# Where the rounded part of a product is subtracted: VectorE in SBUF, or TensorE inside the PSUM bank

## The chip, the cores and the metric

The kernel runs on one core of a Trainium2 chip. Its time is the device time of one execution in microseconds (us). The core has five engines that run their own instruction streams and meet at semaphores: TensorE (PE in the profile, its weight loads PEld), VectorE (DVE), ScalarE (ACT), GpSimd (POOL) and SyncE (SP). TensorE writes its products to PSUM[...]; VectorE and ScalarE read them there.

## The reference

`x` is 16 x 1024 x 256, `adj` a sparse 1024 x 1024 matrix (a few entries per row, the diagonal always). Cut to what matters:

```python
pre_u = einsum('bud,dk->buk', h, W1[:d])
pre_v = einsum('bvd,dk->bvk', h, W1[d:])
S  = sigmoid(einsum('buvk,ko->buvo', relu(pre_u[:, :, None] + pre_v[:, None] + b1), W2)[..., 0] + b2)
a  = einsum('buv,bud->bvd', S * adj, h)
m  = einsum('uv,bud->bvd', adj, h) * h
z  = beta1 * h + beta2 * (a @ Wa + ba) + beta3 * (m @ Wm + bm)
```

Each edge (u, v) has a gate per batch, from the sum of a row of `pre_u` and a row of `pre_v`; the gated and the plain neighbour rows are summed per v and multiplied by two weight matrices.

## The kernel before

**Tiling.** The kernel gathers only existing edges. The batches are 4 groups of 4, the nodes 8 tiles of 128, so there are 32 blocks (group, tile). A block is ten steps, two windows (`w`) of 64 nodes with five lists of 128 edges each. Within a block I count steps from 0 to 9; the code calls the step `s = n % 10` and the block `k = n // 10`. In one step, for 128 edges and 4 batches at once:

- GpSimd fetches the 128 neighbour rows from a table in DRAM (`fetch`, L496), six buffers ahead: 1024 columns of `pre_u` and 1024 of `h`;
- TensorE spreads the block's own `pre_v` rows over the edges, by a 0/1 matrix `mark` (`expand`, L569): `pc = mark.T @ X`, two matmuls of 512 columns. It does so two steps ahead, in two buffers;
- VectorE adds both (`gate`, L601), and applies relu, W2 and the sum over columns, batch by batch (L606, four times);
- ScalarE takes the sigmoid (L609), and scales the edge matrix `left` with it (L612, four times; L579 prepares the next `left`);
- TensorE sums the neighbour rows into accumulators (`aggregate`, L623).

**X and its two parts.** [...] So a row of `pre_v` is stored in two parts: a rounded one and what rounding took away, the low part. `X` is a tile of 128 partitions and two windows. For window 0, partitions 0 to 63 hold the window's rounded rows and partitions 64 to 127 its low parts; for window 1 it is the other way round. `mark` has the one of an edge in both places, so the product adds both parts. `halves(k)` builds `X` for block k while block k - 1 runs:

- per half (512 of 1024 columns) TensorE forms `b1 + h @ w_v` in a PSUM tile `p` (`add_row`, L431, and `half_product`, L427);
- ScalarE copies it to `X` rounded (L461) and to `low` as it is (L462);
- VectorE subtracts the rounded part from `low` (L463), for all 1024 columns at once;
- ScalarE copies the rounded rows of window 1 to their place (L465) and the low parts to theirs (L468, twice).

It is a generator: each `yield` hands on to the next step at which it is called, and those steps are 0, 2, 3, 5 and 6 of block k - 1.

**The order of the work.** It is written out by hand: the main loop (L745) emits each engine's instructions in program order, and `after(step, f)` puts work off to a later step. [...] In a step, TensorE gets the accumulate of the step before, the `expand` for two steps ahead, and then what belongs to this step:

- step 0: half 0 of `halves`; step 1: four transposes of an accumulator (`turn_over`, L641; ScalarE copies the result to `LT`, L644); step 2: half 1;
- steps 3 to 6: the end of the block before (`block_end`: products with `w_a` and `w_m`, L672, copied to `z` by L675);
- steps 7 and 9: transposes again.
- In a list of further steps (`at`, L730), a half of `rows`: `pre_u` of a later group (`w_u`, L427), copied to `tab` by ScalarE (L443) and stored to the table. In blocks 7 to 16 and 18 to 23 one of these is in step 1, behind the transposes and behind what `halves` does there. After block 23 there are none.

**PSUM.** All these products, the transposes, and `p`, live in tiles named `misc` (`small`, L220), for which there are two banks. A new `misc` tile waits until a bank's last reader is done. `pc` and the accumulators have banks of their own.

Of the kernel before, what the change touches and what calls it, by code (L numbers as in the profile page):

```python
# [7 lines left out]
FP = mybir.dt.float32  # L8
FR = mybir.dt.float32r
I32 = mybir.dt.int32  # L10
AF = mybir.ActivationFunctionType
ALU = mybir.AluOpType
AX = mybir.AxisListType
P = 128
# [3 lines left out]
def kernel(  # L18
# [42 lines left out]
    nc = tc.nc  # L61
# [5 lines left out]
    GD = GB * D  # L67
    W = 64
    NW = P // W
# [35 lines left out]
    def fixed(shape, name, dt=FP):  # L105
        return const.tile(shape, dt, name=name)
# [8 lines left out]
    upto = fixed([P, E], "upto")  # L115
# [3 lines left out]
    row = rows32[:, 0:1]  # L119
# [64 lines left out]

    unit = fixed([P, P], "unit", FR)
    nc.vector.tensor_scalar(unit, upto[:, :P], 0.0, None, ALU.is_ge)
    edge = fixed([P, 1], "edge")
    nc.vector.tensor_scalar(edge, inw, 0.0, None, ALU.is_equal)

# [21 lines left out]
    one = main.enter_context(tc.tile_pool(name="one", bufs=1))  # L211
# [8 lines left out]
    def small(name):  # L220
        return psm.tile([P, 512], FP, name="misc")
# [157 lines left out]
    def fetch_val(n):  # L379

        for i, j in wanted[:n]:
            nc.gpsimd.indirect_dma_start(  # L382
                out=val[:, i, j:j + 1], out_offset=None, in_=adj_flat,
                in_offset=bass.IndirectOffsetOnAxis(ap=vidx[:, i, j:j + 1], axis=0),
                bounds_check=N * N - 1, oob_is_err=False)
        del wanted[:n]
# [12 lines left out]
    def after(step, f):  # L399
        due.setdefault(step, []).append(f)  # L400
# [23 lines left out]
    def half_product(p, hT, wt, h, begun):  # L424
        for bb in range(2):
            for i in range(DC):
                nc.tensor.matmul(p[:, bb * D:(bb + 1) * D], hT[:, 2 * h + bb, i, :], wt[:, i, :],  # L427
                                 start=(i == 0 and not begun), stop=(i == DC - 1), skip_group_check=begun)

    def add_row(p, parts):  # L430
        nc.tensor.matmul(p, unit, parts.unsqueeze(1).to_broadcast([P, 2, D]),  # L431
                         start=True, stop=False, skip_group_check=True)
# [18 lines left out]

    def halves(k):
        X = cuts[k] = big.tile([P, NW, GD], FR, name="X")
        low = one.tile([P, GD], FP, name="low")
        for h in range(2):
            step = yield
            c = slice(2 * h * D, (2 * h + 2) * D)
            p = small("p")
            add_row(p, b1_p)
            half_product(p, hTs[order[k]], w_v, h, True)  # L460
            nc.scalar.copy(X[:, 0, c], p)  # L461
            nc.scalar.copy(low[:, c], p)  # L462
        after(step + (2 if k else 1), lambda: nc.vector.tensor_tensor(low, low, X[:, 0, :].bitcast(FP), ALU.subtract))  # L463
        yield
        nc.scalar.copy(X[W:, 1, :], X[W:, 0, :].bitcast(FP))  # L465
        for w in range(NW):
            yield
            nc.scalar.copy(X[(1 - w) * W:(2 - w) * W, w, :], low[w * W:(w + 1) * W])  # L468

    engines = mybir.EngineType  # L470
    main.enter_context(tc.manual_schedule(
# [2 lines left out]
    def do(step):  # L474
        for f in due.pop(step, ()):
            f()
# [10 lines left out]
    BS = NG * NT  # L487
# [6 lines left out]
    def fetch(n):  # L494
        k, g, vt, w, j = where(n)
        nc.gpsimd.indirect_dma_start(  # L496
            out=fetched[n % NF], out_offset=None, in_=table[g],
            in_offset=bass.IndirectOffsetOnAxis(ap=uidx[:, vt * NW + w, j:j + 1], axis=0),
            bounds_check=N - 1, oob_is_err=False)
# [23 lines left out]
    for t, turns_ in enumerate(script):  # L523
        step = t - 100
# [48 lines left out]
    def left_adj(n):  # L573
        k, g, vt, w, j = where(n)
        i = vt * NW + w
        m = len(QUARTERS[j])
        o = max(2 * j - 1, 0)
        lefts[n] = wk.tile([P, 2, GB, 2, V], FP, name="left")
        nc.scalar.activation(lefts[n][:, :m, :, 0, :], onehot[:, i, o:o + m, :].unsqueeze(2).to_broadcast([P, m, GB, V]),  # L579
                             AF.Copy, scale=val[:, i, j:j + 1])  # L580
# [33 lines left out]
    def aggregate(n):  # L614
        k, g, vt, w, j = where(n)
        left, f = lefts.pop(n), fetched[n % NF]
        for i, q in enumerate(QUARTERS[j]):
            h, r = divmod(q, 2)
            first = j == h * MID and r == 0
            if first:  # L620
                accs[h] = psa.tile([P, 2, D], FP, name=f"acc{h}")
            for b in range(GB):
                nc.tensor.matmul(accs[h][b * 2 * V:(b + 1) * 2 * V, r, :],  # L623
                                 left[:, i, b].rearrange("p k v -> p (k v)"), f[:, GD + b * D:GD + (b + 1) * D],
                                 start=first, stop=(j == q + 1), skip_group_check=True)


    def half_end(n, q):

        evs[q] = one.tile([P, 2, D], FP, name=f"ev{q}")  # L630
        nc.scalar.copy(evs[q], accs.pop(q))  # L631
# [113 lines left out]
    for n in range(total + 2):  # L745
        k, s = divmod(n, T)
        if 1 <= n <= total:
            aggregate(n - 1)
            fetch_val(2)
            if n - 1 + NF < total:  # L750
                fetch(n - 1 + NF)
            if n % TW in (0, MID + 1):
                half_end(n - 1, 0 if n % TW else 1)
        if n < total:
            gate(n)
            if n + 1 < total:
                left_adj(n + 1)
        if n % TW == 1 and n // TW + 1 < total // TW:
            load_mark(n // TW + 1)
        do(n)  # L760
        if n + 2 < total:
            expand(n + 2)
        if n == 1:
            w_a = load_weights(Wa, "w_a", nc.sync)
            w_m = load_weights(Wm, "w_m", nc.sync)
            bias = load_rows(bm, D, "bias", nc.sync)
            ba_b = load_rows(ba, D, "ba_b", nc.sync)
            be1 = load_rows(beta1, 1, "be1", nc.sync)
            be2 = load_rows(beta2, 1, "be2", nc.sync)
            be3 = load_rows(beta3, 1, "be3", nc.sync)  # L770
            after(10, scale_late)
        if s == 0 and 0 < k < BS:
            hbs[k - 1] = big.tile([P, GB, D], FP, name="h_blk", bufs=1)
            g, vt = order[k - 1]
            nc.sync.dma_start(hbs[k - 1], x_rows[vt * P:(vt + 1) * P, g * GB:(g + 1) * GB, :])
        if n == total - 6:
            hbs[BS - 1] = hts.tile([P, GB, DC, P], FP, name="hT").rearrange("p b c n -> p b (c n)")
            for v, m, f in tails:
                for h, o in tail_rows(x, v, m, f):
                    nc.sync.dma_start(h, o)  # L780
        for i in advance.get(n, ()):
            next(made[i], None)
        if n in start_list:
            running.append([made[start_list[n]], True, n])
            piece_of(running[-1], n)
        fill(n, False)
        if (s == 1 and 0 < k < BS) or n == total:
            turn_over(k - 1, 1, 1, n)
        if s in (3, 4, 5, 6) and 0 < k < BS:
            if s == 3:  # L790
                end = block_end(k - 1)
                next(end)
            go(end, n)
        if s == 7 and k < BS:
            turn_over(k, 0, 0, n)
            turn_over(k, 0, 1, n)
        if s == 9 and k < BS:
            turn_over(k, 1, 0, n)
        if n == total - 2:
            end = tail(tails[:2], n)  # L800
            next(end)
        elif n == total - 1:
            go(end, n)
        elif n >= total:
            end = tail([tails[2 + n - total]], n)
            next(end)
            go(end, n)
            go(end, n)
        if k + 1 < BS and s in (0, 2, 3, 5, 6):
            if s == 0:  # L810
                parts = halves(k + 1)
                next(parts)
            go(parts, n)
        if n in loads:
            if loads[n] in begun and loads[n][0] == 1:
                aside_.remove(loads[n])
            load_hT(loads[n])
            if loads[n] not in begun:
                copy_h(loads[n])
                begun.add(loads[n])  # L820
        if n in at:
            if at[n] != last:
                last = at[n]
                piece = rows(last)
                next(piece)
            go(piece, n)
        if n == 120:
            nc.gpsimd.partition_all_reduce(longest, rest, P, bass_isa.ReduceOp.max)
            after(n + 12, count_rest)
# [7 lines left out]
    with tc.If(any_left > 0):  # L837
        with ExitStack() as s2:
# [3 lines left out]
            for vt in range(NT):  # L842
# [55 lines left out]
                for b in range(B):  # L898
# [7 lines left out]
                    for k, w in enumerate((w_m, w_a)):  # L906
                        for c in range(DC):
                            nc.tensor.matmul(pz, lt[:, k, c, :], w[:, c, :],
                                             start=(k == 0 and c == 0), stop=(k == 1 and c == DC - 1))
# [34 lines left out]
```

## Time and profile before

| | us |
|---|---|
| median of three runs | 1175.09 |
| lowest, highest | 1167.80, 1177.88 |
| span of the profiled execution | 1165.8 |
| first gate to last gate | 71.6 to 1145.4 |
| a block, by the gates: blocks 0 to 5 | 37.6 to 42.7 |
| blocks 7 to 23 | 31.3 to 37.9 |
| blocks 24 to 30 | 31.3 to 31.9 |

The profiled execution's own time is not given apart from its span; its span lies 9.3 us below the median of the runs and 2.0 below the lowest. A row of the timeline has start, length, engine, line, operation, tiles written and read, shapes and count; in brackets stands how long the engine was idle before it, and which instruction ended that. Matmuls are pipelined: each row's length counts until the last result, so the distance of two starts, not the length, is what one costs TensorE.

### The profile page before, as it was taken

To read this page: it belongs to the slowest core of one execution; us is meant where nothing else is said; L and a number is where in the kernel's file an instruction comes from. 1 tells how busy PE (TensorE), PEld (TensorE's weight loads), DVE (VectorE), ACT (ScalarE), POOL (GpSimd) and SP (SyncE) were. 2 spreads that over 40 slices of the span, in tenths; PEclk is the share of its full clock that TensorE was granted. 3 is DMA by queue.
4 is the path that set the end of the run, shared out by engine and by line. 5 is a ranking of instruction groups with operands and counts; after the bars stand their busy time and mean duration, and the time that the engine had idled before them with its cause. 6 is when DMAs were issued, how large, how long until landed. Compare 5 with 4: busy or idle time off the path is not lost. (4 is left out here: it accounts for less than half of the span.)

```text
span 1165.8 us, 23918 instructions
## 1 busy us (share of the span) xinstructions
PE 1092.1 (94%) x7633; PEld 723.1 (62%) x7633; DVE 1056.2 (91%) x3487; ACT 893.5 (77%) x2624; POOL 439.9 (38%) x428
## 2 busy tenths in 40 slices
PE   7867899999999999999999999999999999999986
PEld 6744666666666666666666666666666666666553
DVE  7688889888999989999999999999999999999994
ACT  2346587767887878888888888888888888888873
POOL 1556645253335333443333333333333333333330
PEclk9868899999999999999999999999999999999999
DMA  9986898999999999999999999999998998999991
GB/s 286 298 307 223 277 372 312 362 320 331 342 320 323 396 379 336 358 350 402 389 374 369 355 364 356 360 364 383 371 375 324 361 322 333 334 339 328 328 346 60
DMA packets 147048, 391.40 MB, mean 336 GB/s; under 512 B 16753, under 2 KB 105329, under 8 KB 110705
## 3 DMA queue, kind: packets, MB, share of 16 engines
q0 software_dynamic: 50016, 300.50, 68.9%
q1 hardware_dynamic: 81616, 74.99, 20.0%
q10 hardware_dynamic: 15280, 14.29, 3.7%
q8 instruction: 63, 1.03, 0.3%
q14 instruction: 73, 0.59, 0.1%
HBM read 393.78 MB, written 50.33 MB: 381 GB/s over the span
## 5 line engine op out<-in xcount | busy, mean ns | idle before, releaser
L496 POOL DMA_INDIRECT fetched<-table,uidx x320 | 341.5, 1067 | 628.3 <-PE acc L623 447.2
L606 DVE SCALAR_TENSOR_TENSOR t<-t,w_b 128x256 f32<-128x256 f32 x1280 | 478.3, 421 | 19.3 <-ACT left L612 0.5
L601 DVE TENSOR_TENSOR t<-fetched,pc 128x1024 f32<-128x1024 f32 x320 | 389.3, 1217 | 41.4 <-PE pc L569 13.9
L623 PE MATMUL acc<-fetched,left 128*32 128x256 f32 x4096 | 336.2, 391 | 31.9 <-ACT left L612 26.2
L612 ACT ACTIVATE left<-left,gt 128x32 f32<-128x32 f32 (+1 forms) x1280 | 299.3, 304 | 10.4
L569 PE MATMUL pc<-X,mark 128*128 128x512 f32 x640 | 237.6, 453 | 6.2 <-ACT mark L562 5.0
L623 PEld LDWEIGHTS acc<-fetched,left 128*32 128x32 f32 x4096 | 130.6, 109 | 179.3 <-issue 52.4
L569 PEld LDWEIGHTS pc<-X,mark 128*128 128x128 f32 x640 | 97.2, 191 | 140.0 <-issue 89.3
L609 ACT ACTIVATE gt<-sc,b_b 128x4 f32<-128x4 f32 x320 | 96.2, 301 | 43.4 <-DVE t L606 40.8
L672 PE MATMUL misc<-w_m,LT 128*128 128x256 f32 x496 | 117.2, 379 | 0.0
L672 PE MATMUL misc<-w_a,LT 128*128 128x256 f32 x496 | 117.1, 379 | 0.0
L579 ACT ACTIVATE left<-onehot,val 128x128 f32<-128x128 bf16 (+1 forms) x320 | 116.5, 364 | 0.0
L427 PE MATMUL misc<-w_v,hT 128*128 128x256 f32 x448 | 107.3, 383 | 0.0
L427 PE MATMUL misc<-w_u,hT 128*128 128x256 f32 x416 | 101.2, 390 | 5.7 <-ACT few L329 3.6
L606 DVE DVE_READ_ACCUMULATOR t<-t,w_b 128x1 f32 x1280 | 104.0, 81 | 0.0
L672 PEld LDWEIGHTS misc<-w_a,LT 128*128 128x128 f32 x496 | 93.9, 189 | 15.1
L672 PEld LDWEIGHTS misc<-w_m,LT 128*128 128x128 f32 x496 | 93.8, 189 | 14.9
L382 POOL DMA_INDIRECT val<-in_adjT_dram,vidx x80 | 85.7, 1071 | 35.1 <-issue 22.4
L427 PEld LDWEIGHTS misc<-w_v,hT 128*128 128x128 f32 x448 | 86.0, 192 | 13.9
L427 PEld LDWEIGHTS misc<-w_u,hT 128*128 128x128 f32 x416 | 79.5, 195 | 17.3 <-ACT few L329 3.7
L631 ACT COPY ev<-acc 128x512 f32<-128x512 f32 x128 | 75.5, 590 | 14.6 <-PE acc L623 4.2
L675 ACT COPY z<-misc 128x512 f32<-128x512 f32 x62 | 36.3, 586 | 58.1 <-PE misc L672 38.8
(164 smaller groups left out, 947.9 us busy)
## 6 DMA issues: line engine op xcount, KB each, us to landing
h_blk<-in_x_dram SPq DMA_DIRECT2D x31, 512.0 KB
out_dram<-z SPq DMA_DIRECT2D x31, 512.0 KB
hT<-in_xT_dram SPq DMA_DIRECT2D x28, 512.0 KB
table<-in_x_dram ACTq DMA_DIRECT2D x24, 512.0 KB
table<-tab SPq DMA_DIRECT2D x24, 512.0 KB
fetched<-table,uidx POOLq DMA_INDIRECT x320
table<-in_x_dram SPq DMA_DIRECT2D x8, 512.0 KB
table<-fetched SPq DMA_DIRECT2D x8, 512.0 KB
```

The source lines that it names most:

```text
L382: nc.gpsimd.indirect_dma_start(out=val[:, i, j:j + 1], out_offset=None, in_=adj_flat, in_offset=bass.IndirectOffsetOnAxis(ap=vidx[:, i, j: ...
L427: nc.tensor.matmul(p[:, bb * D:(bb + 1) * D], hT[:, 2 * h + bb, i, :], wt[:, i, :], start=(i == 0 and not begun), stop=(i == DC - 1), skip ...
L496: nc.gpsimd.indirect_dma_start(out=fetched[n % NF], out_offset=None, in_=table[g], in_offset=bass.IndirectOffsetOnAxis(ap=uidx[:, vt * NW ...
L569: nc.tensor.matmul(pcs[n][:, c], marks[n // TW][:, j * P:(j + 1) * P], cuts[k][:, w, c], start=True, stop=True)
L579: nc.scalar.activation(lefts[n][:, :m, :, 0, :], onehot[:, i, o:o + m, :].unsqueeze(2).to_broadcast([P, m, GB, V]), AF.Copy, scale=val[:, ...
L601: nc.vector.tensor_tensor(t, fetched[n % NF][:, :GD].rearrange("p (b d) -> p b d", b=GB), pcs.pop(n).rearrange("p (b d) -> p b d", b=GB), ...
L606: nc.vector.scalar_tensor_tensor(t[:, b, :], t[:, b, :], 0.0, w2_b, ALU.max, ALU.mult, accum_out=sc[:, b:b + 1])
L609: nc.scalar.activation(gt, sc, AF.Sigmoid, bias=b2_b)
L612: nc.scalar.activation(lefts[n][:, :m, b, 1, :], lefts[n][:, :m, b, 0, :], AF.Copy, scale=gt[:, b:b + 1])
L623: nc.tensor.matmul(accs[h][b * 2 * V:(b + 1) * 2 * V, r, :], left[:, i, b].rearrange("p k v -> p (k v)"), f[:, GD + b * D:GD + (b + 1) * D ...
L631: nc.scalar.copy(evs[q], accs.pop(q))
L672: nc.tensor.matmul(pz[:, bb * D:(bb + 1) * D], LTs[k][:, c, 2 * h + bb, i, :], wt[:, c, :], start=False, stop=(i == 0 and c == DC - 1), sk ...
```

## The change

The subtraction moves to TensorE. A constant matrix `minus`, the identity times -1 in fp32r, is made once. For each half, ScalarE copies `p` to `X` rounded, as before, and at once copies the rounded rows of window 1 to their place. One step later TensorE multiplies the rounded `X` by `minus` and adds the product to `p` in its bank, which leaves the low part there; ScalarE copies that from PSUM to its two places. `low` and VectorE's subtraction are gone. The steps at which `halves` is called become 0, 1, 2 and 3.

```diff
     unit = fixed([P, P], "unit", FR)
     nc.vector.tensor_scalar(unit, upto[:, :P], 0.0, None, ALU.is_ge)
+    minus = fixed([P, P], "minus", FR)
+    nc.vector.tensor_scalar(minus, upto[:, :P], row, -1.0, ALU.is_equal, ALU.mult)
...
     def halves(k):
         X = cuts[k] = big.tile([P, NW, GD], FR, name="X")
-        low = one.tile([P, GD], FP, name="low")
         for h in range(2):
-            step = yield
+            yield
             c = slice(2 * h * D, (2 * h + 2) * D)
             p = small("p")
             add_row(p, b1_p)
             half_product(p, hTs[order[k]], w_v, h, True)
             nc.scalar.copy(X[:, 0, c], p)
-            nc.scalar.copy(low[:, c], p)
-        after(step + (2 if k else 1), lambda: nc.vector.tensor_tensor(low, low, X[:, 0, :].bitcast(FP), ALU.subtract))
-        yield
-        nc.scalar.copy(X[W:, 1, :], X[W:, 0, :].bitcast(FP))
-        for w in range(NW):
+            nc.scalar.copy(X[W:, 1, c], X[W:, 0, c].bitcast(FP))
             yield
-            nc.scalar.copy(X[(1 - w) * W:(2 - w) * W, w, :], low[w * W:(w + 1) * W])
+            nc.tensor.matmul(p, minus, X[:, 0, c], start=False, stop=True, skip_group_check=True)
+            for w in range(NW):
+                nc.scalar.copy(X[(1 - w) * W:(2 - w) * W, w, c], p[w * W:(w + 1) * W])
...
-        if k + 1 < BS and s in (0, 2, 3, 5, 6):
+        if k + 1 < BS and s in (0, 1, 2, 3):
             if s == 0:
                 parts = halves(k + 1)
                 next(parts)
             go(parts, n)
```

## The prediction

> **What bounds the kernel now.** I read the totals first.
>
> ```profile
> PE 1092.1 (94%) x7633; PEld 723.1 (62%) x7633; DVE 1056.2 (91%) x3487; ACT 893.5 (77%) x2624; POOL 439.9 (38%) x428
> ```
>
> TensorE and VectorE are both nearly full, so the totals name no bound. I cut the span into blocks. One block is ten gather steps, and the 32 blocks are not alike: up to block 23, most blocks also compute two halves of `rows` (the `w_u` products); after that none does. Two windows, one block each: number 20 (with `rows`) and number 27 (without). Columns: length, then busy time of PE, weight loads, DVE, ACT, POOL, then clock, DMA share, GB/s.
>
> ```profile
> 772.50:804.60 32.10, 32.10 (x234) 21.45 (x233) 30.95 (x96) 27.26 (x82) 10.47 (x11) 1.00 1.01 382
> 993.90:1025.20 31.30, 30.16 (x218) 19.19 (x217) 30.15 (x96) 26.36 (x80) 10.50 (x11) 1.00 0.90 328
> ```
>
> In block 20 TensorE has no idle time. In block 27 both have some, so the timeline must decide. TensorE, from the bias row of block 21 (804.58) to the `w_u` product in its step 1, and on:
>
> ```profile
> 804.58 0.39 PE L431 MATMUL misc<-b_p,unit 128*128 128x512 f32 x1
> 804.81 1.89 PE L427 MATMUL misc<-w_v,hT 128*128 128x256 f32 x8
> 806.63 0.64 PE L623 MATMUL acc<-fetched,left 128*32 128x256 f32 x8
> 807.20 0.73 PE L569 MATMUL pc<-X,mark 128*128 128x512 f32 x2
> 807.77 0.60 PE L641 MATMUL misc<-ident,ev 128*128 128x128 f32 x4
> 808.20 1.89 PE L427 MATMUL misc<-w_u,hT 128*128 128x256 f32 x8
> 810.02 1.07 PE L623 MATMUL acc<-fetched,left 128*32 128x256 f32 x16
> ...
> 836.54 0.40 PE L431 MATMUL misc<-b_p,unit 128*128 128x512 f32 x1
> ```
>
> Each group starts before the one ahead has ended: packed. The same row returns 31.96 us later, and that is TensorE's own pace here. Adding start distances gives about the same: accumulates 4 x 0.57 + 6 x 1.00, pc pairs 10 x 0.57, `w_v` halves 2 x 2.05, block end 7.7, transposes 2.0, `w_u` 2 x 1.82: 31.4. Without `rows` it is 27.8, some 3.5 below block 27's 31.3. There VectorE sets the pace:
>
> ```profile
> 1037.47 0.42 DVE L606 SCALAR_TENSOR_TENSOR t<-t,w_b 128x256 f32<-128x256 f32 x1
> 1037.82 0.08 DVE L606 DVE_READ_ACCUMULATOR t<-t,w_b 128x1 f32 x1
> 1037.82 1.22 DVE L463 TENSOR_TENSOR low<-low,X 128x1024 f32<-128x1024 f32 x1
> 1038.95 1.21 DVE L601 TENSOR_TENSOR t<-fetched,pc 128x1024 f32<-128x1024 f32 x1
> ```
>
> The subtraction to be removed stands between two gates without a gap and takes 1038.95 - 1037.82 = 1.13. So TensorE bounds blocks 7 to 23 (looser in 7, 9, 10, 11, which also build neighbour lists), VectorE bounds 24 to 30, and blocks 0 to 5 (37 to 43 us each) are bound by neither alone.
>
> ScalarE between the end of `w_v` and the `LT` copy will matter:
>
> ```profile
> 806.74 0.58 ACT L461 CAST X<-misc 128x512 fp32r<-128x512 f32 x1 [0.50 <-PE misc L427]
> 807.22 0.59 ACT L462 COPY low<-misc 128x512 f32<-128x512 f32 x1
> 807.70 0.31 ACT L609 ACTIVATE gt<-sc,b_b 128x4 f32<-128x4 f32 x1
> 808.04 0.96 ACT L612 ACTIVATE left<-left,gt 128x32 f32<-128x32 f32 x4
> 808.90 0.39 ACT L579 ACTIVATE left<-onehot,val 128x128 f32<-128x128 bf16 x1
> 809.19 0.71 ACT L562 CAST mark<-whose 128x640 fp32r<-128x640 uint8 x1
> 809.80 0.57 ACT L644 COPY LT<-misc 128x512 f32<-128x512 f32 x1
> 810.28 0.58 ACT L443 COPY tab<-misc 128x512 f32<-128x512 f32 x1
> ```
>
> It starts only when `w_v` has ended (0.50 us of wait) and then runs without a gap, so the `LT` copy ends at 810.37, 5.8 us after the bias row, whatever TensorE does meanwhile.
>
> [...]
>
> **The change, part by part.**
>
> *Subtraction leaves VectorE* (L463, one per block): -1.13 a block where VectorE is the bound, nothing where TensorE is.
>
> *ScalarE copies.* Before, per block: four at 0.59 (L461, L462), three at 1.045 (L465, L468): 5.5. [...] ScalarE isn't full; only order counts. In step 0 the X-to-X copy takes L462's place[...] and loses the 0.1 overlap as it waits for the cast: +0.15 on the chain above. The low copies of half 0 now stand behind step 1's `LT` copy, ahead of the `tab` copy and the next gate: +1.1 there. The next accumulate has that much room where `w_u` follows; elsewhere it costs at most 0.2.
>
> *Two matmuls with `minus`* (128x512 fp32r, once per half, waiting for the cast): no row before has this operation, the nearest is the first of a pc pair. By the pc pair of 0.57 less a second matmul's 0.23 (804.81 - 804.58) it holds TensorE 0.34, and 0.09 more for the accumulate that must start behind a wait (1.82 from eight matmuls' start to the accumulate, against 8 x 0.216, which is (1.89 - 0.379) / 7 each): 0.43. Bounds: 0.23, weights loaded ahead[...]. I take 0.43. In blocks 24 to 30 half 0's lies in an idle 0.59 before the accumulate at 1029.62, half 1's in VectorE's shadow.
>
> *The bank.* This decides. There are two `misc` banks. Before, half 0's product was free once L462 had read it (807.81), and `w_u` of step 1 took that bank with no wait. Now it stays occupied until the low copies, behind `minus`. From the instruction order of the changed kernel: `w_u` of step 1 takes the other bank, which the transposes just ahead have filled, and waits for their `LT` copy. That is so in blocks 7 to 16 and 18 to 23: 16. The copy ends at 810.37 + 0.15 and I allow 0.1 to wake: `w_u` starts at 810.6, not 808.20: +2.4, with half 0's `minus` inside. Queued behind it are the accumulate of step 1, pc for step 4 (so VectorE two steps on), and half 1. Half 1's bank wait (low copies of half 0, done by 811.7) has passed by then. So 2.4 + 0.43 = 2.8 a block, with no idle left to take it.
>
> *Moved steps.* Half 1's copies move from steps 5 and 6 to step 3 and wait for `minus` behind `w_a`. The next gate's sigmoid is about 1.1 later, the accumulate still finds its left ready. No DMA is in the moved steps. The `tab` store on SP's queue follows its copy, 2.4 late; what is queued behind (block loads, z stores, hT) has a block to spare. POOL's fetches shift with the accumulates.
>
> *Sum:* 16 x 2.8 = +45. Blocks 7, 9, 10, 11 had idle TensorE time, half hidden: -6. Block 23 has a second `w_u`, in step 3, behind half 1's low copies (0.3 + 2 x 0.59): +1.5. Blocks 24 to 30: 7 x -1.0 = -7. Blocks 0 to 5: 0.86 more TensorE, 1.13 less VectorE, later banks: between -0.5 and +1.5 each, I take +3 in all. Blocks 6, 17 and the prologue: 0. Total +37: a span of 1203 for 1166. The profiled execution lies 9 us below the runs' median; I add the difference to the median: 1175 + 37 = **1212**.
>
> **Rivals.** *VectorE is the bound throughout* and TensorE's packing an effect of modelled ends: 31 x -1.13 = -35, 1140. For it: 91% busy. Against: block 20's TensorE pace is slower than VectorE's 30.95 busy. 4%. *The wait on the bank is hidden*, through TensorE getting slack elsewhere: 16 x 0.86 = +14, +3, -7: 1185. Against: no gap to be found in block 21. 9%. *The late copies compound*: the later gates (1.1 each) delay accumulates in 23 blocks as well: +37 + 25: 1237. For it: ScalarE is chained to TensorE twice per block. 12%. The side that would make it faster is the first rival: it decides once TensorE has more than those 2.8 us a block to spare. My forecast: 75%.
>
> **How the numbers follow.** Cost bounds: `minus` 0.23 to 0.65 over the 17 uses that no wait hides, -3 to +4; the wait 2.2 to 2.9, -3 to +8; blocks 0 to 5, -6 to +6; idle time, ±6. Together about 1198 to 1227; to leave out no more than a fifth I widen it to 1193 to 1230. Some 1% is what a measurement can tell from no change. Faster by more 3%, within 8%, slower 89%.
>
> **What would show it.** In the profile after: L463's VectorE group gone, VectorE's share down to 85%; `w_u` in step 1 of blocks 7 to 16 and 18 to 23 idle about 2 us before it, released by the `LT` copy; such blocks 34.5 to 35 long, blocks 24 to 30 about 30.3. It is wrong if `w_u` starts behind `minus` without a gap, or if blocks 24 to 30 get longer.

## The result, and the profile after

| | before | after |
|---|---|---|
| median of the runs beside each other, us | 1172.95 | 1201.55 |
| lowest, highest | 1166.21, 1177.88 | 1190.69, 1210.99 |
| span of the profiled execution | 1165.8 | 1195.1 |

The ratio is 1.0244, 95% interval 1.0209 to 1.0279: slower, and inside the forecast range (1193 to 1230), at 1202 instead of 1212. In a second pair of runs, in another session, it was 1.0292 [1.0263, 1.0320]. The kernel before itself took 1170 to 1173 us in some sessions and 1149 in others, so below I compare ratios and the lengths of blocks, not microseconds of different sessions.

Totals and two groups of the profile after (columns as in the forecast: busy us and mean ns of one, then idle us just before them and what ended most of it):

```profile
PE 1097.1 (92%) x7697; PEld 723.9 (61%) x7697; DVE 1023.0 (86%) x3456; ACT 882.0 (74%) x2656; POOL 433.0 (36%) x428
...
L600 DVE TENSOR_TENSOR t<-fetched,pc 128x1024 f32<-128x1024 f32 x320 | 389.8, 1218 | 104.7 <-PE pc L568 70.8
...
L429 PE MATMUL misc<-w_u,hT 128*128 128x256 f32 x416 | 106.9, 406 | 36.5 <-ACT LT L643 25.5
```

VectorE's share fell to 86%, near the announced 85%, but VectorE didn't finish earlier: it now waits for `pc` (70.8 us, 13.9 before). The `w_u` products had 5.7 us of idle time before them in the whole kernel before, and have 36.5 now, mostly ended by the `LT` copy. The waits of the profile after, of weight loads and matmuls (us in total, times, longest):

```profile
PEld misc L429 <- ACT LT L643: 34.1, 14, 2.5
PE misc L429 <- ACT LT L643: 29.8, 14, 2.1
```

Three blocks of the profile after, 20 and 21 (with `rows`) and 26 (without):

```profile
793.36:827.60 34.24, 32.11 (x236) 21.18 (x235) 29.20 (x94) 26.99 (x83) 10.71 (x11) 1.00 1.00 357
827.60:863.39 35.79, 33.67 (x235) 21.70 (x234) 29.20 (x94) 26.98 (x83) 10.69 (x11) 0.95 0.93 329
...
993.40:1024.20 30.80, 30.45 (x229) 19.38 (x221) 29.14 (x96) 26.20 (x82) 10.33 (x10) 1.00 0.93 336
```

Block 20 is 34.24 long, with 2.13 us in which TensorE is idle; I had announced 34.5 to 35. Block 26 is 0.5 shorter than before; five of the others from 24 to 30 are 0.8 to 0.9 shorter, and the seven take 30.4 to 30.8 where I had announced 30.3. Block 21 is longer than block 20 by 1.55 and its clock is below 1: that was not foreseen, and has its own section. TensorE and ScalarE at the bank, timeline of the profile after from the bias row of block 20:

```profile
793.36 0.39 PE L433 MATMUL misc<-b_p,unit 128*128 128x512 f32 x1
793.59 1.89 PE L429 MATMUL misc<-w_v,hT 128*128 128x256 f32 x8
...
796.55 0.60 PE L640 MATMUL misc<-ident,ev 128*128 128x128 f32 x4
796.90 0.47 PE L465 MATMUL misc<-X,minus 128*128 128x512 f32 x1
799.51 0.70 PE L429 MATMUL misc<-w_u,hT 128*128 128x256 f32 x2 [2.13 <-ACT LT L643]
```

```profile
795.52 0.59 ACT L462 CAST X<-misc 128x512 fp32r<-128x512 f32 x1 [0.50 <-PE misc L429]
796.14 0.62 ACT L463 CAST X<-X 64x512 fp32r<-64x512 f32 x1
796.78 0.30 ACT L608 ACTIVATE gt<-sc,b_b 128x4 f32<-128x4 f32 x1
...
798.88 0.57 ACT L643 COPY LT<-misc 128x512 f32<-128x512 f32 x1
799.48 1.17 ACT L467 CAST X<-misc 64x512 fp32r<-64x512 f32 x2
```

The `LT` copy ends at 799.45 and `w_u` starts at 799.51, 6.15 after the bias row, where it stood at 808.20 - 804.58 = 3.62 before. It is late in all 16 blocks, in both traces of the changed kernel: 6.14 to 6.17 after the bias row, and 6.9 in block 7. The low copies of half 0 (L467) come only behind the `LT` copy; until they have read it, half 0's bank is taken.

**Where the time went**, by the spans between gates, trace against trace:

| | forecast | first pair | second pair |
|---|---|---|---|
| start, and blocks 0 to 6 | +3 | -7.3 | -10.1 |
| blocks 7 to 16 | about +22 | +23.2 | +25.4 |
| block 17 | 0 | -2.1 | -1.7 |
| blocks 18 to 23 | about +18 | +21.1 | +21.1 |
| blocks 24 to 30 | -7 | -6.1 | -5.9 |
| span | +37 | +29.3 | +28.9 |

The forecast is split by its own terms: 10 x 2.8 - 6 for blocks 7 to 16, 6 x 2.8 + 1.5 for blocks 18 to 23, together 40; measured are 44.3 and 46.5.

### The profile page after: what moved, and what is told of

The parts are those of the page before. It is cut to its first block, busy times and chain, and to the rows that moved or that the text cites. A ratio compares the mean times of both kernels' runs of the same rounds, so it can differ in the third digit from the quotient of the medians.

```text
span 1195.1 us, 24054 instructions
## 1 busy us (share of the span) xinstructions
PE 1097.1 (92%) x7697; PEld 723.9 (61%) x7697; DVE 1023.0 (86%) x3456; ACT 882.0 (74%) x2656; POOL 433.0 (36%) x428
## 3 DMA queue, kind: packets, MB, share of 16 engines
q8 instruction: 63, 1.03, 0.4%
## 5 line engine op out<-in xcount | busy, mean ns | idle before, releaser
L495 POOL DMA_INDIRECT fetched<-table,uidx x320 | 336.3, 1051 | 665.3 <-PE acc L622 497.6
L600 DVE TENSOR_TENSOR t<-fetched,pc 128x1024 f32<-128x1024 f32 x320 | 389.8, 1218 | 104.7 <-PE pc L568 70.8
L622 PE MATMUL acc<-fetched,left 128*32 128x256 f32 x4096 | 320.2, 392 | 19.0 <-ACT left L611 10.3
L622 PEld LDWEIGHTS acc<-fetched,left 128*32 128x32 f32 x4096 | 119.3, 110 | 164.3 <-issue 65.6
L429 PE MATMUL misc<-w_u,hT 128*128 128x256 f32 x416 | 106.9, 406 | 36.5 <-ACT LT L643 25.5
L429 PEld LDWEIGHTS misc<-w_u,hT 128*128 128x128 f32 x416 | 81.2, 200 | 53.7 <-ACT LT L643 29.3
L643 ACT COPY LT<-misc 128x512 f32<-128x512 f32 x128 | 71.5, 583 | 23.6 <-PE misc L640 13.2
L467 ACT CAST X<-misc 64x512 fp32r<-64x512 f32 x128 | 74.2, 580 | 17.6 <-PE misc L465 12.6
```

What stands on the lines that cost most here:

```text
L467: nc.scalar.copy(X[(1 - w) * W:(2 - w) * W, w, c], p[w * W:(w + 1) * W])
L495: nc.gpsimd.indirect_dma_start(out=fetched[n % NF], out_offset=None, in_=table[g], in_offset=bass.IndirectOffsetOnAxis(ap=uidx[:, vt * NW ...
L600: nc.vector.tensor_tensor(t, fetched[n % NF][:, :GD].rearrange("p (b d) -> p b d", b=GB), pcs.pop(n).rearrange("p (b d) -> p b d", b=GB), ...
L622: nc.tensor.matmul(accs[h][b * 2 * V:(b + 1) * 2 * V, r, :], left[:, i, b].rearrange("p k v -> p (k v)"), f[:, GD + b * D:GD + (b + 1) * D ...
```

## The experiments

Each ratio is to the kernel before in the same session. "Packed pace" is the distance of half 0's bias row from one packed block to the next, where the clock didn't drop. I take it from blocks 8, 12, 13, 15 and 19 to 22: 31.95 to 31.97 in the kernel before in both sessions (once 32.04), 34.23 to 34.25 in the changed kernel.

**1. Hold the bank, and change nothing else.** The kernel before, with half 0's second copy one step later, behind the `LT` copy. No `minus`, and VectorE still subtracts.

```diff
             nc.scalar.copy(X[:, 0, c], p)
+            if h == 0 and k:
+                yield
             nc.scalar.copy(low[:, c], p)
...
-        if k + 1 < BS and s in (0, 2, 3, 5, 6):
+        if k + 1 < BS and s in (0, 1, 2, 3, 5, 6):
```

> The kernel before, with one line moved: the copy of half 0's product to `low` is emitted in step 1, behind the LT copy, so that its PSUM bank is given back late and w_u of step 1 has to take the bank of the transposes, as in the changed kernel. No minus matmul, VectorE's subtraction stays. If the wait on the bank is the cost: w_u in step 1 starts about 2.2 us later in 16 blocks and the time rises by 30 to 45 us, to 1203 to 1218. If TensorE's added matmuls are the cost: within 6 us of the kernel before. If the late ScalarE copies are: about +10.

Measured: 1204.94 us, ratio 1.0297 [1.0231, 1.0363]; packed pace 33.8 to 34.0, blocks 24 to 30 as before. TensorE of this kernel:

```profile
804.69 0.60 PE L643 MATMUL misc<-ident,ev 128*128 128x128 f32 x4
806.88 1.99 PE L427 MATMUL misc<-w_u,hT 128*128 128x256 f32 x8 [1.59 <-ACT LT L646]
```

`w_u` starts 5.37 after the bias row (801.51), 1.75 later than before and not the 2.2 that I expected: ScalarE has one copy less to do ahead of the `LT` copy than in the changed kernel, and ends it 5.32 after the bias row instead of 6.09. The wait is there without any `minus`. It costs 1.84 of the 2.27 us in a packed block; the total loss is as large as that of the whole change because here blocks 24 to 30 gain nothing. So a bank that stays occupied past the `LT` copy is enough for most of the loss.

**2. Take the matmuls out, and leave the bank as it is.** The changed kernel without the line of `minus`.

```diff
-            nc.tensor.matmul(p, minus, X[:, 0, c], start=False, stop=True, skip_group_check=True)
```

> The changed kernel without the two minus matmuls of a block; the low copies stay where they are and read the bank as w_v left it. It leaves out part of the computation: the low part then holds the whole product. Theory of the held bank: the bank is held by the low copies and w_u still waits for the LT copy, so half 0's matmul lay inside that wait and only half 1's 0.23 is saved in each packed block: 16 x 0.23 = 4, some 1 to 4 more in the other blocks, time 1193 to 1200, packed blocks about 34.0. Rival, that the matmuls are what costs (0.43 x 2 a block or more, with the weights behind a wait): 16 x 0.86 = 14 or more below the changed kernel, 1187 or less.

Measured: 1179.28 us against 1149.45, ratio 1.0256 [1.0229, 1.0283], between the two ratios of the changed kernel and above what I allowed. The packed pace is 34.00 to 34.02, so the two matmuls cost 0.23 of the 2.27. A window of one block, and the group:

```profile
782.24:816.24 34.00, 31.64 (x234) 20.83 (x233) 29.20 (x95) 27.00 (x84) 10.70 (x10) 1.00 0.98 353
```

```profile
L429 PE MATMUL misc<-w_u,hT 128*128 128x256 f32 x416 | 106.9, 406 | 39.8 <-ACT LT L642 33.3
```

`w_u` starts 6.14 after the bias row here too (792.50 and 786.36); without half 0's `minus` the idle before it is 2.36 instead of 2.13. Of the few us that I expected to be saved, the traces show 3.5 in blocks 7 to 23 (against the changed kernel's second trace); the start and blocks 0 to 6 lost 3.2, so the time doesn't show it.

**3. Keep the matmuls, and take the wait away.** The changed kernel with `w_u` of step 1 done in step 4 (blocks 7 to 16 and 18 to 22), when banks are free.

```diff
-    ((60 + 10 * i, 68 + 10 * i, 71 + 10 * i) for i in range(NT))
+    ((60 + 10 * i, 68 + 10 * i, 74 + 10 * i) for i in range(NT))
-    ((141, 149, 151), (149, 158, 161), *((153 + 10 * i, 161 + 10 * i, 168 + 10 * i)
+    ((141, 149, 154), (149, 158, 164), *((153 + 10 * i, 164 + 10 * i, 168 + 10 * i)
...
```

> The changed kernel, with the w_u product of step 1 done in step 4 instead, in the packed blocks 7 to 16 and 18 to 22 (block 23 as it was). Nothing else is moved: the minus matmuls, the low copies behind the LT copy and the order on ScalarE ahead of them stay. Theory of the held bank: w_u then finds a bank long free, so the idle of about 2.1 us ahead of it goes, the clock drops with it, and only the two minus matmuls (0.23 to 0.43 each) remain: packed blocks 32.2 to 32.8 us, blocks 24 to 30 about 30.5, time 1160 to 1175. Rival, that the extra work itself (minus and ScalarE's later copies) costs the time: packed blocks stay at 33.4 or more, time 1190 or more.

**4. Its control**, the same edit of the kernel before.

> Control: the kernel before with the same move of w_u from step 1 to step 4. Both theories: within about 6 us of the kernel before, 1165 to 1177, packed blocks 31.8 to 32.3 us. If it is much faster or slower, the move has an effect of its own, and the run of the changed kernel with the move is to be read against this one.

Measured: number 3 took 1156.72 us, ratio 1.0068 [1.0051, 1.0084], packed pace 32.78 to 32.83; number 4 took 1164.59, ratio 1.0139 [1.0069, 1.0209], packed pace 32.67 to 32.69. With the wait gone, 1.44 of the 2.27 us a block is gone, and with this plan every run of the changed kernel (1156.5 to 1157.0) is below every run of its control (1159.3 to 1175.0). But the control lost 0.7 a block, which I had not expected, so both ratios end above what I allowed. TensorE of number 3 and then of number 4 shows why:

```profile
797.46 0.60 PE L640 MATMUL misc<-ident,ev 128*128 128x128 f32 x4
797.81 0.47 PE L465 MATMUL misc<-X,minus 128*128 128x512 f32 x1
798.39 1.68 PE L622 MATMUL acc<-fetched,left 128*32 128x256 f32 x16
800.01 0.73 PE L568 MATMUL pc<-X,mark 128*128 128x512 f32 x2
```

```profile
807.36 0.60 PE L641 MATMUL misc<-ident,ev 128*128 128x128 f32 x4
808.00 1.68 PE L623 MATMUL acc<-fetched,left 128*32 128x256 f32 x16
809.61 0.73 PE L569 MATMUL pc<-X,mark 128*128 128x512 f32 x2
```

In the kernel before the accumulate of step 1 takes 1.00 from start to start, here 1.62 and 1.61: its `left` isn't ready. In the trace of number 4 ScalarE finishes the four parts of `left` at 807.95, 808.16, 808.37 and 808.58, and the first matmul that uses each part starts 0.05 later. While `w_u` stood ahead of this accumulate it covered that. So the move has a price of its own, and only the difference of the two kernels belongs to the change: number 3 reaches the `pc` pair 0.29 later than number 4 (5.74 and 5.45 after their bias rows, 794.27 and 804.16), and over the whole block it is 0.1 behind (a gain of 0.58 behind step 7 is in this, see "No idle left" below).

**5. Is VectorE the bound?** The kernel before without L463.

```diff
-        after(step + (2 if k else 1), lambda: nc.vector.tensor_tensor(low, low, X[:, 0, :].bitcast(FP), ALU.subtract))
```

> The kernel before without the VectorE subtraction of L463, and nothing in its place. It leaves out part of the computation: the low part then holds the whole product. Theory (TensorE bounds blocks 7 to 23, VectorE blocks 24 to 30): packed blocks unchanged within 0.2 us, blocks 24 to 30 shorter by 0.8 to 1.1 each, time 6 to 14 us below the kernel before, 1157 to 1165. Rival (VectorE is the bound throughout): 31 x 1.13 = 35 less, 1135 to 1140, packed blocks 30.8.

Measured: 1140.03 us against 1149.45, ratio 0.9922 [0.9894, 0.9949]. Blocks 21 and 27:

```profile
792.29:824.26 31.97, 31.97 (x233) 21.18 (x232) 29.21 (x96) 27.22 (x82) 10.68 (x11) 1.00 0.99 375
981.70:1012.17 30.47, 29.87 (x217) 18.99 (x218) 29.16 (x96) 26.14 (x80) 10.48 (x10) 1.00 0.94 335
```

VectorE's busy time fell by about 1.0 in both; the packed pace stayed at 31.95 to 31.97, and block 27 gave 0.83 of the 1.13. Without its subtraction on VectorE the whole kernel is 0.8% faster.

**6. `minus` and the low copies ahead of the gate.** The changed kernel, with steps 1 and 3 of `halves` emitted before the step's gate, so that half 0's bank comes free ahead of the `LT` copy.

```diff
+        if k + 1 < BS and s in (1, 3):
+            go(parts, n)
         if n < total:
             gate(n)
...
-        if k + 1 < BS and s in (0, 1, 2, 3):
+        if k + 1 < BS and s in (0, 2):
```

> The changed kernel with each minus matmul and its two low copies emitted earlier in steps 1 and 3: on TensorE between the accumulate and expand, on ScalarE ahead of the gate's sigmoid. Same instructions, other order. w_u of step 1 then takes half 0's own bank. If the wait on the bank is the cost: w_u starts about 4.5 us after the bias row of half 0 (3.6 before, 6.15 in the changed kernel), and the time falls to 1165 to 1182. If the added matmuls or the number of ScalarE copies are the cost: it stays at 1195 to 1205.

Measured: 1193.26 us, ratio 1.0201 [1.0164, 1.0238]. A miss: I had expected 1165 to 1182, hardly a loss, and the time lies just below the range of the rival. TensorE of this kernel, from the bias row at 789.05:

```profile
793.70 1.99 PE L429 MATMUL misc<-w_u,hT 128*128 128x256 f32 x8 [0.46 <-ACT X L467]
...
803.11 1.69 PE L622 MATMUL acc<-fetched,left 128*32 128x256 f32 x16
804.72 0.50 PE L568 MATMUL pc<-X,mark 128*128 128x512 f32 x1
```

`w_u` starts 4.65 after the bias row, nearly where I had put it, and the clock never drops in blocks 7 to 23. Yet packed blocks take 33.4 and blocks 24 to 30 even 31.9. The low copies stand ahead of the sigmoid now. In step 1 it starts at 793.67, 4.62 after the bias row, against 3.12 in the kernel before; there the later `w_u` covers it. In step 3 nothing does: the four parts of `left` end at 803.06 to 803.69, and the accumulate of 803.11 takes 1.61 instead of 1.00. The loss of 1.4 in this block is then the sum of 1.03 for the later start of `w_u`, 0.10 as it takes longer, 0.24 for half 1's `minus` and 0.61 for this accumulate, less 0.58 that the changed kernel gains too (see "No idle left" below).

**7 and 8. Four idle copies on ScalarE, before the gate or behind it.** To test what a copy ahead of the sigmoid does, the kernel before with copies that only take ScalarE's time. In number 7 they stand ahead of the gate in steps 1 and 3; number 8 has the same two lines behind everything else of ScalarE that decides here, the `LT` copy included.

```diff
...
+    def idle_copies():
+        for i in range(4):
+            nc.scalar.copy(spare, upto[:W, :256])
...
+        if k + 1 < BS and s in (1, 3):
+            idle_copies()
         if n < total:
             gate(n)
```

> The kernel before, with four more ScalarE copies of 64x256 [...] ahead of the gate in steps 1 and 3 of every block; they only write a spare tile. No bank is held and no matmul added. If the place of the copies explains the early variant (low copies ahead of the gate's sigmoid delay every left of that step, and the accumulate waits for it): packed blocks 32.8 to 33.6 us, blocks 24 to 30 longer by 0.3 to 0.9 each, ratio 1.012 to 1.025. If instead the early variant lost its time to the minus matmuls or to the bank: packed blocks 32.0 to 32.3, ratio below 1.006.

> The kernel before, with the same four copies in the same steps 1 and 3, but behind the step's gate and behind the LT copy, where the changed kernel has its low copies. Theory of the held bank: there they delay only the tab copy and, a little, the next gate: packed blocks 31.9 to 32.4, ratio 0.997 to 1.006. Rival, that the late copies compound (each later sigmoid delays an accumulate): packed blocks 33 or more, ratio 1.012 or more.

Measured: number 7, 1196.45 us against 1149.64, ratio 1.0410 [1.0384, 1.0436]; packed pace 33.44, blocks 24 to 30 32.97. Number 8, 1155.83, ratio 1.0061 [1.0044, 1.0077]; packed pace 32.07 to 32.39. The accumulates of number 7, then a packed block of number 8:

```profile
L627 PE MATMUL acc<-fetched,left 128*32 128x256 f32 x4096 | 357.3, 390 | 44.5 <-ACT left L616 44.3
```

```profile
788.23:820.62 32.39, 32.39 (x233) 21.60 (x232) 30.37 (x97) 30.14 (x90) 11.01 (x11) 1.00 1.01 369
```

The same four copies, twice a block, cost 1.5 ahead of the gate and 0.1 to 0.4 behind it. Ahead of it, the accumulates of steps 1 and 3 take 1.61 and 1.62 in a packed block instead of 1.00, as that of step 3 does in number 6. So the place of the copies accounts for this part of number 6, and most likely for its loss in blocks 24 to 30. That both have nearly the same packed pace is chance, as `w_u` starts on time in number 7. The idle copies start 0.44 apart, so four take 1.7 us, which is more than two low copies (1.17 in the profile after, L467 at 799.48). Both ratios are above what I allowed, probably in part for this: number 8 by a hair, number 7 mainly as blocks 24 to 30 lost 1.7 each and not 0.3 to 0.9. Number 8 speaks against the rival of the compounding late copies.

**9. Keep the clock up.** The changed kernel with eight matmuls by a zero matrix ahead of half 0's `minus` in the 16 blocks; they lie within the wait.

```diff
...
             yield
+            for i in range(8 if h == 0 and k - 1 in HELD else 0):
+                nc.tensor.matmul(p, nought, X[:, 0, c], start=False, stop=False, skip_group_check=True)
             nc.tensor.matmul(p, minus, X[:, 0, c], start=False, stop=True, skip_group_check=True)
```

> The changed kernel with eight more matmuls by a matrix of zeros into half 0's bank, ahead of minus, in the 16 blocks where w_u waits: TensorE works while it would stand idle, and adds nothing. If the idle 2.1 us is what makes TensorE's clock drop to half for 3.4 us in seven of those blocks: no drop between blocks 7 and 23, 8 to 13 us less than the changed kernel, so 1188 to 1194. If the drops have another cause: as the changed kernel, or up to 5 us more.

Measured: 1188.55 us, ratio 1.0170 [1.0132, 1.0209]. The packed pace is 34.23 to 34.27 without a drop of the clock, and `w_u` still waits for the `LT` copy:

```profile
791.55 2.08 PE L469 MATMUL misc<-X,nought 128*128 128x512 f32 x8
793.47 0.39 PE L470 MATMUL misc<-X,minus 128*128 128x512 f32 x1
794.16 1.99 PE L431 MATMUL misc<-w_u,hT 128*128 128x256 f32 x8 [0.30 <-ACT LT L648]
```

`w_u` starts 6.15 after the bias row (788.01), exactly as in the changed kernel, so the wait is the same and only the clock differs. Blocks 7 to 23 are 10.3 and 7.4 us shorter than in the two traces of the changed kernel: more work made the kernel faster.

**10. Each way where it is good.** The old `halves` in blocks 7 to 16 and 18 to 23, the new one in all others.

```diff
...
+    HELD = (*range(7, 17), *range(18, 24))
...
-        if k + 1 < BS and s in (0, 1, 2, 3):
+        if k + 1 < BS and s in ((0, 2, 3, 5, 6) if k in HELD else (0, 1, 2, 3)):
             if s == 0:
-                parts = halves(k + 1)
+                parts = (halves_old if k in HELD else halves)(k + 1)
```

> The old way of making X in blocks 7 to 16 and 18 to 23, the new way in all others. If the loss lies in those 16 blocks alone and the others gain: blocks 24 to 30 about 30.5 long, the others as before, time 1153 to 1163. If the shorter blocks 24 to 30 only repay what was lost ahead of them: 1170 to 1176.

Measured: 1160.69 us against 1170.22, ratio 0.9918 [0.9891, 0.9946]: faster than both kernels. Blocks 21 and 27:

```profile
801.80:833.20 31.40, 31.40 (x231) 20.66 (x230) 30.22 (x96) 26.75 (x80) 10.45 (x10) 1.00 1.01 378
991.16:1021.66 30.50, 30.16 (x222) 19.13 (x218) 29.19 (x96) 25.96 (x81) 10.21 (x10) 1.00 0.93 340
```

**11 and 12. Both kernels in one session**, for a second pair of traces.

> The kernel before, unchanged, with a trace taken in one chip session with the next one. The times of the kernel before lay at 1170 to 1173 in two sessions and at 1149 in two others. If that comes from the start and blocks 0 to 6, the packed blocks stay at 31.96 and blocks 24 to 30 at 31.3, and the span differs only ahead of block 7. If it comes from a slower TensorE or from the DMAs throughout, the packed blocks move too.

> The changed kernel, unchanged, in one session with the one above, so that its trace can be set against a trace of the same session: packed blocks 34.23, or 35.8 where the clock drops, blocks 24 to 30 about 30.5, ratio 1.021 to 1.028; the difference of the two spans in blocks 7 to 23 about 40 us.

Measured: 1149.66 (ratio 1.0003 [0.9985, 1.0021]) and 1183.40 (1.0292 [1.0263, 1.0320]; a trifle above what I wrote). In the trace of 1155.0 against the first one of 1165.8 the packed pace is the same 31.95 and blocks 18 to 30 agree within 0.2; 1.8 of the 10.8 us lies ahead of the first gate, 3.4 in blocks 0 to 6 and 5.0 in blocks 7 to 16, there mainly in 7 to 9, 12, 14 and 15. Why the sessions differ wasn't tried further. The start and blocks 0 to 6 vary by about as much from trace to trace as the change could move them.

## Why the prediction was right, point by point

**The bound by blocks** was read rightly. Number 5 shows it: taking VectorE's subtraction away moves no packed block and gives 6.3 us in blocks 24 to 30 (6.1 against the second trace of the kernel before). The changed kernel gains 6.1 and 5.9 there against my 7: I gave 1.0 of the 1.13 per block, and 0.83 is typical.

**The bank** was the right mechanism. It is shown from three sides: holding it alone gives the loss (1), taking the matmuls out leaves it (2), moving `w_u` away from it ends most of it (3). The wait is 2.53 longer in the trace against the 2.4 predicted: the `LT` copy ended 6.09 after the bias row, not 5.94. What I had added for the X-to-X copy on this chain, 0.15, was an estimate; it is 0.30. That copy (L463 in the profile after) takes 0.62 and starts 0.03 after the cast's end, and the sigmoid starts 0.02 after the copy's end; L462 took 0.59, started 0.10 before the cast's end, and the sigmoid 0.11 before its own.

**`minus`** was oversized where it isn't hidden: 0.43 taken, 0.23 measured, which was my lower bound; the upper one, 0.65, was an estimate that no row of a trace showed. Half 1's, in the profile after:

```profile
806.85 1.89 PE L671 MATMUL misc<-w_a,LT 128*128 128x256 f32 x8
808.39 0.58 PE L465 MATMUL misc<-X,minus 128*128 128x512 f32 x1
808.90 1.07 PE L622 MATMUL acc<-fetched,left 128*32 128x256 f32 x16
```

From `w_a` to the accumulate it takes 2.05, against 1.82 before. The cast had ended 2.6 us before, and the trace shows no wait ahead of it.

**"No idle left to take it" was the step that failed.** I added start distances to 31.4, saw a pace of 31.96, and called that about the same. The 0.56 was a wait. In the second pair of traces, the transposes of step 7 and what follows, first the kernel before, then the changed one:

```profile
785.92 1.03 PE L641 MATMUL misc<-ident,ev 128*128 128x128 f32 x8
786.89 1.65 PE L623 MATMUL acc<-fetched,left 128*32 128x256 f32 x16
788.47 0.73 PE L569 MATMUL pc<-X,mark 128*128 128x512 f32 x2
```

```profile
809.15 1.03 PE L640 MATMUL misc<-ident,ev 128*128 128x128 f32 x8
810.12 1.07 PE L622 MATMUL acc<-fetched,left 128*32 128x256 f32 x16
811.12 0.73 PE L568 MATMUL pc<-X,mark 128*128 128x512 f32 x2
```

That accumulate took 1.58 before and takes 1.00 now. A row of grouped matmuls counts a wait inside it as busy (the length grows from 1.07 to 1.65), so the window showed 32.10 busy of 32.10. It waited for `left`. ScalarE at this place, first the kernel before, then the changed one:

```profile
785.07 1.05 ACT L468 CAST X<-low 64x1024 fp32r<-64x1024 f32 x1
786.14 0.30 ACT L609 ACTIVATE gt<-sc,b_b 128x4 f32<-128x4 f32 x1
```

```profile
807.69 0.59 ACT L674 COPY z<-misc 128x512 f32<-128x512 f32 x1 [1.38 <-PE misc L671]
808.17 0.30 ACT L608 ACTIVATE gt<-sc,b_b 128x4 f32<-128x4 f32 x1
```

Before, the second low copy of `halves`, in step 6, stands right ahead of this sigmoid; the change moved it to step 3. The four parts of `left` ended at 786.80 to 787.43 before, the last three when the accumulate had begun (786.89); now they end at 808.82 to 809.46, ahead of 810.12. The other traces show that the place of this copy decides and not the stop at the bank: in the packed blocks the accumulate takes 1.57 to 1.58 in all eight traces with the old place, number 1 with its stop included, and 1.00 in all six with the new one, number 3 without a stop included. The paragraph on moved steps counted what half 1's copies would delay in step 3, and put at nothing what they would free in step 6. Moving only these copies, and leaving the bank as it was, wasn't tried.

So per packed block, in these two traces: 2.52 for the later start of `w_u`, 0.10 as its weights are loaded behind a wait (1.93 for the eight instead of 1.83; in the first pair the first weight load starts at 799.50, 0.01 ahead of its product, and at 808.10, 0.10 ahead, in the kernel before), 0.23 for half 1's `minus`, less 0.58: 2.27, against 2.8 predicted. Over 16 blocks that is 8.5 us less.

**The clock** brought this back, and more. In each of the two traces of the changed kernel seven drops of 3.4 us fall into blocks 7 to 23, none in those of the kernel before. At 1.55 each that is 10.9 us which no step of the forecast had. So the sum for blocks 7 to 23 came out close partly by luck: 2.27 a block and a clock penalty, in place of 2.8.

**Smaller items.** Block 23, with its second wait in step 3, has +3.5 (36.69 for 33.21), +4.3 predicted. Of the looser blocks, 9 and 10 hid most of it (+0.2, and +0.8 once 1.55 for a drop of the clock is taken off, in the second pair), but 7 hid nothing (+2.8), and 11 differed between the pairs. Block 17 gained 2 us, where I had put 0: it has no `w_u` in step 1, and VectorE seems to bound it like blocks 24 to 30 (number 5 gained 1.2 and 0.7 there against the two traces). For blocks 0 to 5 I put +3, and the traces say -1.4 and -7.7; two traces of the changed kernel differ by 9.7 there, so this is no finding. The late copies do not compound (8); ahead of the gate they would delay accumulates (6, 7).

## What to carry to other kernels

Before a step is moved off a busy engine, ask how long each PSUM bank it touches stays taken, and which product takes that bank next: here a 0.2 us matmul cost little, and the copies that released its bank behind another copy cost 2.5 us of TensorE in each of the 16 blocks. When copies move, count also what they free in the place that they leave: here 0.58 in each packed block. When the sum of start distances is half a microsecond below the pace, look for the wait, and don't trust a busy share of 100% that is made of grouped matmuls. And where a kernel has stages with different bounds, an edit can be right in one and wrong in another: left out of the 16 blocks where `w_u` needs the bank, this one is worth 0.8%.

## What the hardware showed that was not expected

**Behind a pause of 2.1 us TensorE's clock was a half for 3.4 us, in seven of 16 blocks.** Around block 21's `w_u`, the profile after:

```profile
831.14 0.47 PE L465 MATMUL misc<-X,minus 128*128 128x512 f32 x1
833.73 2.47 PE L429 MATMUL misc<-w_u,hT 128*128 128x256 f32 x8 [2.12 <-ACT LT L643]
836.14 1.94 PE L622 MATMUL acc<-fetched,left 128*32 128x256 f32 x16
```

The pause is that of block 20, but the sixteen matmuls behind it take 1.86 from start to start instead of 1.00; the recorded clock is 0.50 from 835.11 to 838.52, and 1.00 all through block 20. In this trace the seven drops of blocks 7 to 23 start at 347.00, 384.55, 456.23, 596.17, 729.29, 835.11 and 869.24; each lasts 3.41, and their distances are whole multiples of 3.413 us. I laid stretches of that length, counted from the drops, over the matmul records. Block 20's pause (797.37 to 799.51) had 1.95 us in one stretch, the one from 797.56, and no drop followed; block 21's (831.61 to 833.73) had 2.04 in the one from 831.69, and the drop came as that one ended. So with two pauses of nearly one length, 2.13 and 2.12, the second block took 1.55 us more, and what differed was where the pause fell on this grid. In blocks 7 to 23 of four traces (the changed kernel twice, numbers 1 and 2), of the stretches in which TensorE had no matmul for 2.00 us or more, 19 of 19 were followed by one at half clock; of those with 1.79 to 1.95 us, 5 of 15; of those with less, none. In the profile after alone these are 6 of 6, 1 of 6 and none. The ends of matmuls are modelled, so the lengths are good to perhaps 0.1 us. That filling the pause keeps the clock up is shown by number 9, which had no drop there; how long a pause has to be is read from these traces alone, and wasn't varied.
